# Four graph layers in one kernel: the recurrent layer's state is turned by DMA and VectorE instead of TensorE, two groups' recurrences are woven, and ScalarE takes the score's two addends

## The chip, the cores and the metric

The kernel runs on one core of a Trainium2 chip. The core has five engines that run side by side, each through its own list of instructions in the order of the list: TensorE (PE in the profile; PEld is its weight load), VectorE (DVE), ScalarE (ACT), GpSimd (POOL) and SyncE (SP), which here issues all DMA transfers. An instruction that needs a result of another engine waits, and all that stands behind it on its own engine waits with it. The metric is the device time of one execution in microseconds (us). The kernel before took 2698.12 us, the median of three runs (2695.11 to 2700.67).

## The reference

Input are 128 graphs with 128 nodes each, node rows `x` (128, 128, 256) in fp32 and an adjacency `adj` (128, 128, 128) in int32 that holds zeros and ones. Four layers follow one another, each as `x = layernorm(x + layer(x, adj))`:

```python
# layer 0: attention with 4 heads of 64
Wh = (X @ W).reshape(B, N, H, F)
e = leaky_relu(e_src[:, :, None, :] + e_dst[:, None, :, :], 0.2)   # e_src, e_dst: Wh against a_src, a_dst
alpha = softmax(where(mask, e, NEG_INF), axis=2)
Hout = elu(einsum('bijh,bjhf->bihf', alpha, Wh))
# layer 1: three rounds of a gated recurrent cell over the graph
for i in range(3):
    m = h @ weight[i]
    aggr = einsum('bst,bsd->btd', A, m)
    h = gru_cell(aggr, h, w_ih, w_hh, b_ih, b_hh)     # r, z: sigmoid; n: tanh(i_n + r*h_n); (1-z)*n + z*h
# layer 2: one weight for each relation 1..4 of adj, plus a bias
# layer 3: attention with one head of 256, as layer 0
```

The graphs are independent of one another.

## The kernel before

Graphs are handled in 33 groups: one of two graphs, 31 of four and one of two. For a group of four a tile is [128 partitions, 4 x 128 or 4 x 256].

**Stages and lanes.** Each group passes through generators, and one step of a generator is what it issues up to its next `yield`. `head` (letter h in the tables of the order) is layer 0; `reset_and_new` (p) and `new_and_update` (q) write the products of the recurrent gates; `chunk_0` and `chunk_1` (u and v) do the rest of the recurrent layer for the lower and upper 128 of the 256 state columns; `tail` (t) does layers 2 and 3; `loads` (l) fetches inputs; `constants` and `fold` (c, f) prepare weights at the start.

**The recurrent layer.** The state is kept transposed, state columns on partitions and nodes along the row: tiles `hT`, one for each half of the columns. A gate of four graphs needs a product of a 2 x 2 block matrix of weights with a 2 x 2 block matrix of states; it is done with seven block products instead of eight (the factors `f[0]` to `f[6]` on the weights, and sums `T_h`, `T_a` of state blocks made by `right_sums`, L559). One such product, L603, is written as one matmul of 128 x 256 and runs as two TensorE instructions. The gates r, ni, nh and z share three PSUM banks of the tag `sums` and three of `gate`; two banks of the tag `ps` serve all else.

For the neighbours (`neighbours`, L577) the product with the adjacency (`edge`) contracts over nodes, so it needs the state with nodes on partitions. After rounds 1 and 2 each half of the new state `hT` is therefore turned. Before the change TensorE does that for every group (`"gru": tuple(range(64))` in `BY_PE`): four transposes of 128 x 128 into one `ps` bank (L127), and a ScalarE copy to `hN` (L699). Then come four neighbour products, a ScalarE copy `agT` (L586) and VectorE differences `T_a`.

**Turning by DMA.** Elsewhere in the middle groups a tile is turned by DMA: one write to a DRAM scratch (`to_dram`), four reads that fetch 32 x 32 squares to their mirrored places (`squares`, pieces of 128 bytes), and a VectorE transpose within each 32 x 32 square. So are turned x0 (L450), the probabilities `em` to `aT` (L525, L840), `h0T`, the last state (tail, L730 and L737) and `x3T`. `BY_PE` names the first and last groups that use TensorE for this instead.

**Scores.** In layer 0 the destination scores of a group are turned into rows in DRAM (`to_rows`, L414 and L416) and read back spread over all partitions straight into `em` (`from_rows`, L424). VectorE then adds, for each graph and head, the own score (a column of `wh`) and the mask `nbias` in one instruction (L488, 16 for a group of four), and the softmax follows on `em`. `nbias` is -1e30 where there is no edge; VectorE makes it from `adj` (L433), once for layer 0 and once for layer 3, where `adj` is loaded a second time (`adj3`, L154).

**The order.** All instructions are issued in an order written out by hand in strings: `START`, then `STEPS` once for each of the 29 middle positions p, then `END`. Each letter stands for one step of one stage of a group at a distance from p (the tables `FIRST`, `PERIOD`, `LAST`). At the end of the function every instruction is tied to its predecessor on the same engine, so each engine, SP with its DMA issues too, follows the strings. In one period of `STEPS` nearly all recurrent work is of one group: of the 72 steps each of p and q, 68 and 67 are of group p, 4 and 5 of group p-1.

Of the kernel before, what the change touches and what calls it, by code (L numbers as in the profile page):

```python
# [9 lines left out]
F32 = mybir.dt.float32  # L10
BF16 = mybir.dt.bfloat16
I32 = mybir.dt.int32
# [4 lines left out]
P = 128  # L17
# [9 lines left out]
BY_PE = {"head": (0,), "rows0": (0, 1), "gru": tuple(range(64)), "rows3": (-1,), "tail": (-1, -2)}  # L27
# [26 lines left out]
FIRST = {"a": ("h", 0), "b": ("c", 0), "c": ("f", 0), "d": ("l", 1), "e": ("h", 1), "f": ("l", 0), "g": ("p", 0), "h": ("u", 0), "i": ("q", 0), "j": ("v", 0), "k": ("l", 2), "l": ("h", 2), "m": ("u", 1), "n": ("v", 1), "o": ("p", 1), "p": ("q", 1), "q": ("t", 0), "r": ("l", 3), "s": ("h", 3)}  # L54
START = """
aababbcbcaccaaccaadccacacacaccacaadaacccccccaeaaaacaacaaaaaaaaaaaeecaaaceaaeaeaeaeeaafcacaaeeaaaaghh
dcigjfchjibhggicjgijiejjigeggcgckgeeigeiggcggiigbjgeihiiigigghicjeeiigehgjgiheigiehejiechjhijccciejh
ghjihechkjiclbjjhgejihhihgiejigjggjijgiggigfjiggeigilegjighgeieggciejghiggiigehhiilhejigeehgeheejhlj
lijheigihjhiieejhjhjijhjjgieghjgejgjggeegijegliegiebgfghlgiilggigjlhgilhiggigilgiijhigejliiglhhigijl
jiiejmnminnmopjnomonnhohoplojoqoopopplpopmlpoopoqolqobnppqoooolpqpmpqopqpllmpnpmmppqoqpnoqmopqmqmmfm  # L60
dpopnqqplqnmmlnplnonmrnnmqprlqnomnlnpspopqolpqpnolqnpqqpqnnolqooopqpoqlopbpompoqnqplsplolopopsolonpm
opnommmloqmsmllloslqmmpoqpqmnmnkmpnlqnmqllqqnoopqmmnnonnnqqqosolqpspslsnploplnnqllpoolosoqnoooplsqpp
monpooppopponosommlnppppp
"""
PERIOD = {"a": ("q", -1), "b": ("p", -1), "c": ("u", -1), "d": ("h", 0), "e": ("u", 0), "f": ("v", 0), "g": ("t", -2), "h": ("h", 1), "i": ("l", 2), "j": ("v", -1), "k": ("p", 0), "l": ("h", 2), "m": ("q", 0), "n": ("t", -1), "o": ("l", -1), "p": ("t", -3), "q": ("l", 0), "r": ("l", 1)}
STEPS = """
abbcdccebfeaegefaahibjcfahkcjjkfjgilkfkkfmjmkkmkkmknmhkkmmhmkmekemfgkkmnhfmmkmkhfekkmomkhnmegmhkmkgm
mkennnengeggenhmekmenmennpnfennhenhfmmhkfemnfekffnfnnhhffmqkfmnflmmknmnffhkkkgnkmhgfmmkknkmpnmgmlhek
khhngfhfgnkmekmhkemkmhmpnmkhkkglmghnkelefenmlehhnhkmhlrnkemffnekehhffnnefhnfmefnefmnfneekkfhkhgmkhpf
mmfnhlkkfhkkfmkmmkmhlkknmmlkhnmehlgmemlffkknmkefmmnkkkmm  # L70
"""
LAST = {"a": ("t", -2), "b": ("p", -3), "c": ("q", -3), "d": ("u", -3), "e": ("h", -2), "f": ("v", -3), "g": ("h", -1), "h": ("u", -2), "i": ("v", -2), "j": ("p", -2), "k": ("t", -4), "l": ("t", -5), "m": ("q", -2), "n": ("t", -3), "o": ("l", -3), "p": ("t", -1), "q": ("l", -1), "r": ("l", -2), "s": ("u", -1), "t": ("v", -1), "u": ("p", -1), "v": ("q", -1)}
END = """
abbccdbdcdbedfgfhijfcihdhhikiclfjjjmjmjijgljfmgjjlmimmjjmmgjmhknjkmjjijmmkigmimnhjmhggjgmnmjmjhmghmg
nkkmnhjnnhggjhkjghnmkhnhmjhnnmjiniimnnihklgnhmikkhmngnniikininjmnnmiiijmnmgmoiipmnjjnjjjkgmjmjjnnkmq
gmgjjmihhpgjigjimjgmmgjjajmhgmjjngmhmjghnhmnhmgjnmighghghirniniihnhiijnhngnmmhgihikjnjijmnjimigkmgjn
gjgjijmnjimmjjmmkjgmhhjmiimghmgmjjmnirmjjnjjmmjgstjmnjmjnhmhtsimthisthmsuuiuuitvtuvvuuuvuhivuvauuuav
vusktuauuvsvavanvvvuuvnsvvutnvuasvvksnvuntusvvsnuvassnususaaatsataatnssasvvttaaaavtvtatantvtuututuuu
taukvnuvnvtauauavvavqvvauuntkvuvnnsvusuvvvuvauutauvusasautsunsvtastaavnstsasvsuatstatsttvtusqtauvsvu
tuaavtvuututnuvuvvvusuvuvsavutvvutvuvuavsuauuvvuvsusvvuatussavtttasavttppnaappppaappapppppppppppnpap  # L80
pappnapppappppppppppppappappppppapappapapaapppppppppp
# [8 lines left out]
def kernel(ctx: ExitStack, tc: tile.TileContext, a: dict, out: bass.AP):  # L90
# [43 lines left out]
    negone = cp.tile([P, 1], F32, tag="negone", name="negone")  # L134
    nc.gpsimd.memset(negone, -1.0)

    unmet = cp.tile([P, NG], F32, tag="unmet", name="unmet")
# [13 lines left out]

    def load_adj_again(st):
        st["adj3"] = sp.tile([P, st["n"], N], I32, tag="adj3", name=f"adj3_{st['g']}")
        nc.sync.dma_start(st["adj3"], adj[st["graphs"]].rearrange("g n m -> n g m"))  # L154
# [14 lines left out]
    def loads(st):  # L169
        for load in (load_x_squares, load_adj, load_rows, load_adj_squares, load_adj_again):  # L170

            if st["g"] != 0 or load in (load_adj_squares, load_adj_again):
                load(st)
            yield
# [256 lines left out]
    def absent(adj_t, name):  # L431
        nbias = ring(sp, [P, adj_t.shape[1], N], F32, "nbias", f"nbias_{name}", 2)
        nc.vector.tensor_scalar(nbias, adj_t, 0.0, NEG, ALU.is_le, ALU.mult)  # L433
        return nbias


    def head(st):
# [14 lines left out]
        nbias = absent(st["adj"], f"0_{g0}")  # L452
        yield
        if st["relations"] < R:
            above = sp.tile([P, n, N], F32, tag="rel", name=f"above_{g0}")
            nc.scalar.activation(above, st["adj"], AF.Relu, bias=negone, accum_out=unmet[:, g0 : g0 + 1])
# [16 lines left out]
        for k in range(0, G, 2):  # L473
            if k >= n:
                for _ in range(7):
                    yield
                continue
            em = ring(sp, [P, 2, H, N], F32, "em", f"em0_{g0}_{k}", 2)
            raw = {}
            for g in range(k, k + 2):  # L480
                if alone:
                    raw[g] = from_rows(bank(H, N), rows, range(g * H, g * H + H))
                else:
                    raw[g] = from_rows(em[:, g - k], rows[g])
            yield
            for g in range(k, k + 2):
                for h in range(H):
                    nc.vector.scalar_tensor_tensor(  # L488
                        em[:, g - k, h, :],
                        raw[g][:, h, :],  # L490
                        wh[:, g, D + h : D + h + 1],
                        nbias[:, g, :],
                        ALU.add,
                        ALU.add,
                    )
                yield
            blocks = em.rearrange("p g h n -> p (g h) n")
            yield from softmax_unscaled(blocks, nm, den, slice(k * H, (k + 2) * H))
            ems[k] = em if by_pe else to_dram(f"em0_{g0}_{k}", blocks)
            yield  # L500
        aTs = {}
        for k in range(0, G, 2):
            if k < n:
                aTs[k] = ring(sp, [P, 2, H, N], F32, "aT", f"aT0_{g0}_{k}", 2)
# [3 lines left out]
        y = ring(sp, [P, n, D], F32, "x1", f"x1_{g0}", 2)  # L508
# [32 lines left out]
        st["edge"] = ring(sp, [P, n, N], F32, "edge", f"edge_{g0}", 2)  # L541
# [101 lines left out]
    def chunk(st, c):  # L643

        g0, G = st["g"], st["n"]
        for l, layer in enumerate(st["layers"]):
# [34 lines left out]
            if l + 1 < L:  # L681

                by_pe = st["by_pe"]["gru"]
# [27 lines left out]
    def tail(st):  # L711
# [86 lines left out]
        nbias = absent(st["adj3"], f"3_{g0}")  # L798
# [27 lines left out]
        aT = sp.tile([P, n, N], F32, tag="aT3", name=f"aT3_{g0}")  # L826
# [129 lines left out]
```

## Time and profile before

| | |
|---|---|
| median of three runs | 2698.12 us |
| the profiled execution, its own time | 2696.64 us |
| its span, first to last instruction | 2694.8 us |
| mean granted TensorE clock | 0.992 |
| busy: PE, PEld, DVE, ACT, POOL | 98%, 85%, 81%, 66%, 34% |
| TensorE instructions | 13861 |
| DMA, queue q1: packets, share of 16 engines | 1206252, 58.0% |

Times are from one profiled execution. A busy share is the time in which at least one instruction of the engine runs; matmuls overlap one another, so TensorE's pace is read from the starts of its instructions, not from their durations. A row of a group gives count, busy time in us and mean duration in ns, then the idle time before it and what ended it. A DMA row gives the time from issue to landing.

### The profile page before, as it was taken

The numbers are of one execution on the slowest core, as the hardware profiler recorded it, in microseconds if no ns is written. First come the engines' busy times: TensorE is split into PE (matmuls) and PEld (weight loads), VectorE is DVE, ScalarE is ACT, GpSimd is POOL, SyncE is SP. The second block draws the span as 40 slices with busy tenths as digits, with TensorE's granted clock in tenths as the row PEclk, the third lists the DMA queues.
The fourth block names the chain that finished last, engine by engine and source line by source line (L and its number), as shares of the span: only waits on it lengthen the run. The fifth ranks groups of instructions, "written<-read, shape, count | busy, mean of one in ns | idle before, by whom it ended". The sixth has DMA issues, their size and how long they took to land. (4 is left out here: it accounts for less than half of the span.)

```text
span 2694.8 us, 43276 instructions
## 1 busy us (share of the span) xinstructions
PE 2635.8 (98%) x13861; PEld 2287.6 (85%) x13861; DVE 2187.5 (81%) x5059; ACT 1774.2 (66%) x4510; POOL 915.8 (34%) x923
## 2 busy tenths in 40 slices
PE   8899999999999999999999999999999999999996
PEld 5788888888888888888888888888888888888885
DVE  5777888888888888888888888888888888888875
ACT  3556666667666667766667766667766667766755
POOL 0233434333434333434233434333334333334331
PEclk8999999999999999999999999999999999999998
DMA  3455565666565666575666575665676566565521
GB/s 90 88 108 102 110 126 116 124 115 111 116 133 112 123 116 111 116 132 112 123 118 109 117 132 114 121 119 111 114 131 115 121 117 108 116 131 109 118 46 35
DMA packets 1206486, 302.31 MB, mean 112 GB/s; under 512 B 930156, under 2 KB 1190380, under 8 KB 1206252
## 3 DMA queue, kind: packets, MB, share of 16 engines
q1 hardware_dynamic: 1206252, 299.47, 58.0%
q8 instruction: 113, 1.85, 0.3%
q14 instruction: 121, 0.99, 0.1%
HBM read 192.03 MB, written 107.33 MB: 111 GB/s over the span
## 5 line engine op out<-in xcount | busy, mean ns | idle before, releaser
L603 PE MATMUL gate<-T_h,factors_h 128*128 128x256 f32 (+1 forms) x2376 | 688.4, 374 | 2.8 <-DVE gate L631 2.7
L603 PE MATMUL gate<-T_a,factors 128*128 128x256 f32 (+1 forms) x2376 | 676.8, 373 | 0.5 <-DVE gate L631 0.5
L603 PEld LDWEIGHTS gate<-T_a,factors 128*128 128x128 f32 x2376 | 444.5, 190 | 60.3 <-DVE T_a L566 2.0
L603 PEld LDWEIGHTS gate<-T_h,factors_h 128*128 128x128 f32 x2376 | 434.4, 190 | 69.8 <-issue 12.6
L603 PE MATMUL sums<-agT,factors 128*128 128x256 f32 (+1 forms) x1188 | 336.5, 377 | 1.8 <-DVE sums L623 1.6
L670 POOL TENSOR_TENSOR d<-h1T,n 128x512 f32<-128x512 f32 (+1 forms) x66 | 95.1, 1441 | 487.4 <-ACT n L667 484.8
L393 ACT ACTIVATE em<-em,nm 128x128 f32<-128x128 f32 x640 | 248.4, 398 | 7.7 <-DVE nm L390 7.6
L603 PEld LDWEIGHTS sums<-agT,factors 128*128 128x128 f32 x1188 | 217.5, 190 | 37.6 <-DVE sums L623 10.2
L667 ACT ACTIVATE n<-n,bih 128x512 f32<-128x512 f32 (+1 forms) x198 | 140.5, 709 | 135.8 <-DVE n L665 131.7
L356 ACT ACTIVATE x<-x,mr_x,rs_x 128x256 f32<-128x256 f32 x384 | 202.6, 590 | 28.7 <-DVE mr_x L351 28.7
L740 POOL TENSOR_TENSOR x<-x,x 128x512 f32<-128x512 f32 x61 | 76.5, 1274 | 366.3 <-DVE x L737 366.3
L124 PE MATMUL ps<-wh,aT 128*128 128x64 f32 (+1 forms) x1280 | 192.7, 298 | 3.0 <-DVE aT L840 2.2
L613 ACT COPY sums<-gate 128x256 f32<-128x256 f32 (+1 forms) x396 | 140.8, 355 | 83.2 <-PE gate L603 76.2
L124 PEld LDWEIGHTS ps<-wh,aT 128*128 128x128 f32 x1280 | 172.1, 194 | 21.9 <-DVE aT L840 12.3
L603 PE MATMUL gate<-agT,factors 128*128 128x256 f32 (+1 forms) x594 | 175.1, 376 | 1.1 <-ACT r L655 0.7
L655 ACT ACTIVATE r<-sums,bhalf 128x512 f32<-128x512 f32 (+1 forms) x99 | 66.1, 668 | 158.1 <-PE sums L603 158.1
L466 ACT COPY wh<-ps 128x264 f32<-128x264 f32 x128 | 47.2, 369 | 175.3 <-PE ps L124 175.2
L670 POOL TENSOR_TENSOR d<-h2T,n 128x512 f32<-128x512 f32 (+1 forms) x66 | 82.4, 1249 | 225.5 <-ACT n L667 213.0
L675 DVE SCALAR_TENSOR_TENSOR d<-z,d 128x512 f32<-128x512 f32 (+1 forms) x198 | 138.6, 700 | 25.2 <-POOL d L670 15.9
L349 POOL TENSOR_TENSOR rs_x<-rs_x,neghalf 128x4 f32<-128x4 f32 (+1 forms) x99 | 98.9, 999 | 139.0 <-DVE rs_x L348 128.6
L586 ACT COPY agT<-ps 128x512 f32<-128x512 f32 (+1 forms) x198 | 112.0, 566 | 48.9 <-PE ps L124 48.5
L343 DVE BATCH_NORM_STATS2 st_x<-x 128x6 f32<-128x256 f32 x384 | 139.6, 411 | 4.1
(165 smaller groups left out, 6134.1 us busy)
## 6 DMA issues: line engine op xcount, KB each, us to landing
em<-d_rows SPq DMA_DIRECT2D x153, 256.0 KB, 4.7
d_em<-em SPq DMA_DIRECT2D x63, 512.0 KB, 3.6
aT<-d_em SPq DMA_DIRECT2D x252, 128.0 KB, 4.3
x0s<-in_x_dram SPq DMA_DIRECT2D x248, 64.0 KB, 2.9
adj<-in_adj_dram SPq DMA_DIRECT2D x62, 256.0 KB, 3.6
x<-in_x_dram SPq DMA_DIRECT2D x31, 512.0 KB, 4.6
d_h0T<-x SPq DMA_DIRECT2D x62, 256.0 KB, 3.4
h0T<-d_h0T SPq DMA_DIRECT2D x124, 128.0 KB, 3.8
```

Source lines behind the costliest of these rows:

```text
L124: nc.tensor.matmul(ps, lhsT, rhs, start=start, stop=stop)
L343: nc.vector.bn_stats(sums[:, g, :], y[:, g, :])
L349: nc.gpsimd.tensor_tensor(rs, rs, neghalf[:, :n], ALU.pow)
L356: nc.scalar.activation(y[:, g, :], y[:, g, :], AF.Identity, bias=mr[:, g : g + 1], scale=rs[:, g : g + 1])
L393: nc.scalar.activation(em[:, r, :], em[:, r, :], AF.Exp, bias=nm[:, i : i + 1], accum_out=den[:, i : i + 1])
L586: nc.scalar.copy(t, ps)
L603: nc.tensor.matmul(into, w[:, SEL[name], k - 1], layer[source][k], start=start, stop=True, skip_group_check=True)
L613: nc.scalar.copy(c11, c21)
L667: nc.scalar.activation(n, n, AF.Tanh, bias=bih[:, 2 * C + c : 2 * C + c + 1])
L670: nc.gpsimd.tensor_sub(d, hT, n)
L675: nc.vector.scalar_tensor_tensor(d, tz, 1.0, d, ALU.add, ALU.mult)
L740: nc.gpsimd.tensor_add(y[:, k : k + 2], y[:, k : k + 2], st["x1"][:, k : k + 2])
```

## The change

- `BY_PE`: the key `gru` becomes `gru1` and `gru2`, both with groups 0, 1 and the last two. In the other 29 groups the state after rounds 1 and 2 is turned by the path that the code already had: a write of `hT` to DRAM, four reads in squares to `hN`, a VectorE transpose of 128 x 512.
- Scores of layer 0: ScalarE makes `own` (mask plus own score) by 16 instructions of 128 x 128 for a group of four, from `nbias` and `wh` alone; VectorE adds `own` to the rows with one instruction of 128 x 1024 for two graphs.
- `absent` makes `nbias` on ScalarE, for layer 0 from `adj`, for layer 3 from `edge`, which is kept longer (ring of four). The second load of `adj` goes.
- The test that `adj` holds only zeros and ones uses a Square instead of a Relu.
- `em` and `aT` share one ring of three tiles; `own` has one; `x1` has three; the layer-3 `aT3` takes the place of `em3`.
- `rows0` gets group 2: its score rows are spread by TensorE.
- A new written order. In one period, of p's 72 steps 47 are of group p and 25 of group p-1, of q's 41 and 31: the last round of one group is woven with the first rounds of the next. The tail reaches to group p-4.

```diff
-BY_PE = {"head": (0,), "rows0": (0, 1), "gru": tuple(range(64)), "rows3": (-1,), "tail": (-1, -2)}
+BY_PE = {"head": (0,), "rows0": (0, 1, 2), "gru1": (0, 1, -1, -2), "gru2": (0, 1, -1, -2), "rows3": (-1,), "tail": (-1, -2)}
...
-PERIOD = {"a": ("q", -1), "b": ("p", -1), "c": ("u", -1), "d": ("h", 0), "e": ("u", 0), "f": ("v", 0), "g": ("t", -2), "h": ("h", 1), "i": ("l", 2), "j": ("v", -1), "k": ("p", 0), "l": ("h", 2), "m": ("q", 0), "n": ("t", -1), "o": ("l", -1), "p": ("t", -3), "q": ("l", 0), "r": ("l", 1)}
+PERIOD = {"a": ("v", 0), "b": ("t", -3), "c": ("u", 0), "d": ("q", -1), "e": ("t", -2), "f": ("u", -1), "g": ("p", -1), "h": ("p", 0), "i": ("l", 2), "j": ("v", -1), "k": ("q", 0), "l": ("h", 1), "m": ("l", -1), "n": ("t", -4), "o": ("h", 2), "p": ("l", 1), "q": ("t", -1), "r": ("u", 1)}
 STEPS = """
-abbcdccebfeaegefaahibjcfahkcjjkfjgilkfkkfmjmkkmkkmknmhkkmmhmkmekemfgkkmnhfmmkmkhfekkmomkhnmegmhkmkgm
...
+abcccdeaddfgaehieadihjdkeakahhdfbflhkjdhjffmlnjhhkeelhkhehohfbljhelekjehkhkhcehjjkfcekeeahllefhnklae
...
-    negone = cp.tile([P, 1], F32, tag="negone", name="negone")
-    nc.gpsimd.memset(negone, -1.0)
+    negbig = cp.tile([P, 1], F32, tag="negbig", name="negbig")
+    nc.gpsimd.memset(negbig, NEG)
...
-    def load_adj_again(st):
-        st["adj3"] = sp.tile([P, st["n"], N], I32, tag="adj3", name=f"adj3_{st['g']}")
-        nc.sync.dma_start(st["adj3"], adj[st["graphs"]].rearrange("g n m -> n g m"))
...
-    def absent(adj_t, name):
-        nbias = ring(sp, [P, adj_t.shape[1], N], F32, "nbias", f"nbias_{name}", 2)
-        nc.vector.tensor_scalar(nbias, adj_t, 0.0, NEG, ALU.is_le, ALU.mult)
+    def absent(st, present, name):
+
+        nbias = ring(sp, [P, st["n"], N], F32, "nbias", f"nbias_{name}", 2)
+        if st["relations"] < R:
+            nc.scalar.activation(nbias, st[present], AF.Identity, bias=negbig, scale=-NEG)
+        else:
+            if present != "adj":
+                load_adj(st)
+            nc.vector.tensor_scalar(nbias, st["adj"], 0.0, NEG, ALU.is_le, ALU.mult)
         return nbias
...
-            above = sp.tile([P, n, N], F32, tag="rel", name=f"above_{g0}")
-            nc.scalar.activation(above, st["adj"], AF.Relu, bias=negone, accum_out=unmet[:, g0 : g0 + 1])
+            off = sp.tile([P, n, N], F32, tag="rel", name=f"off_{g0}")
+            nc.scalar.activation(off, st["adj"], AF.Square, bias=neghalf[:, :1], accum_out=spread[:, g0 : g0 + 1])
...
-            em = ring(sp, [P, 2, H, N], F32, "em", f"em0_{g0}_{k}", 2)
-            raw = {}
-            for g in range(k, k + 2):
-                if alone:
-                    raw[g] = from_rows(bank(H, N), rows, range(g * H, g * H + H))
-                else:
-                    raw[g] = from_rows(em[:, g - k], rows[g])
+            em = ring(sp, [P, 2, H, N], F32, "em", f"em0_{g0}_{k}", 3)
+            own = ring(sp, [P, 2, H, N], F32, "own", f"own_{g0}_{k}", 1)
+            if not alone:
+                for g in range(k, k + 2):
+                    from_rows(em[:, g - k], rows[g])
             yield
             for g in range(k, k + 2):
                 for h in range(H):
-                    nc.vector.scalar_tensor_tensor(
-                        em[:, g - k, h, :],
-                        raw[g][:, h, :],
-                        wh[:, g, D + h : D + h + 1],
-                        nbias[:, g, :],
-                        ALU.add,
-                        ALU.add,
+                    nc.scalar.activation(
+                        own[:, g - k, h, :], nbias[:, g, :], AF.Identity, bias=wh[:, g, D + h : D + h + 1]
                     )
                 yield
+            if alone:
+                for g in range(k, k + 2):
+                    raw = from_rows(bank(H, N), rows, range(g * H, g * H + H))
+                    nc.vector.tensor_add(em[:, g - k], raw, own[:, g - k])
+            else:
+                nc.vector.tensor_add(em, em, own)
+            yield
...
-                aTs[k] = ring(sp, [P, 2, H, N], F32, "aT", f"aT0_{g0}_{k}", 2)
+                aTs[k] = ring(sp, [P, 2, H, N], F32, "em", f"aT0_{g0}_{k}", 3)
...
-        st["edge"] = ring(sp, [P, n, N], F32, "edge", f"edge_{g0}", 2)
+        st["edge"] = ring(sp, [P, n, N], F32, "edge", f"edge_{g0}", 4)
...
-                by_pe = st["by_pe"]["gru"]
+                by_pe = st["by_pe"]["gru" + "12"[l]]
...
-        nbias = absent(st["adj3"], f"3_{g0}")
+        nbias = absent(st, "edge", f"3_{g0}")
```

## The prediction

> **What bounds the kernel now.** First the page's head and the stretch from 300 to 2300 us, where one period of the order follows another.
>
> ```profile
> span 2694.8 us, 43276 instructions
> PE 2635.8 (98%) x13861; PEld 2287.6 (85%) x13861; DVE 2187.5 (81%) x5059; ACT 1774.2 (66%) x4510; POOL 915.8 (34%) x923
> ...
> 300.00:2300.00 2000.00, 1989.84 (x10410) 1739.55 (x10410) 1666.97 (x3811) 1354.30 (x3410) 708.85 (x695) 1.00 0.62 118
> ```
>
> In the middle TensorE is busy 99.5% at full granted clock (1.00), VectorE 83%, ScalarE 68%, the DMA engines 62%. A busy share of overlapping matmuls could hide holes, so I went on to TensorE's timeline and read the starts.
>
> ```profile
> 973.29 0.59 PE L603 MATMUL gate<-T_h,factors_h 128*128 128x256 f32 x2
> 973.72 0.59 PE L603 MATMUL gate<-T_a,factors 128*128 128x256 f32 x2
> ...
> 976.33 0.60 PE L127 MATMUL ps<-ident,h2T 128*128 128x128 f32 x4
> 976.76 0.60 PE L603 MATMUL gate<-h2T,factors_h 128*128 128x256 f32 x2
> ```
>
> A recurrent product (two instructions) takes 0.43 us from start to start, and so do four transposes of a state half. At these spacings I count 79.2 us of TensorE for a group of four: 126 products 54.4, the projections with x0s, x3T and hr 10.5, the attention products of both layers 5.3, neighbours 5.4, relations 1.8, state transposes 1.73. The layer-3 probabilities of successive groups are turned (L840) at 201.0 to 2615.8 us in 31 instructions, 80.5 us apart. So TensorE has only some 1.4 us of holes a period: its work is the time. Of the waits of TensorE for others, the longest in all are small and scattered:
>
> ```profile
> PEld gate L603 <- PE gate L603: 16.9, 28, 0.6
> PEld sums L603 <- DVE sums L623: 16.5, 44, 1.3
> ...
> PEld ps L124 <- DVE aT L840: 12.3, 28, 0.9
> ```
>
> **The transposes of the recurrent state.** 29 groups lose four sets of four transposes: 29 x 4 x 0.435 = 50.5 us less TensorE work. Their copies (L699, 585 ns) go from ScalarE: -2.3 us a group, all beside TensorE. In their place each set gets one DMA write, four reads and a VectorE transpose of 128 x 512. The trace has exactly this shape in layer 3:
>
> ```profile
> d_h<-h3T SPq DMA_DIRECT2D x60, 256.0 KB, 2.4
> aT<-d_em SPq DMA_DIRECT2D x120, 64.0 KB, 2.2
> ...
> L840 DVE STREAM_TRANSPOSE aT<-aT 128x512 f32<-128x512 f32 x30 | 20.8, 694 | 0.0
> ```
>
> A turn of one half: the write lands in 2.4 us and the reads follow 2.7 us after it (the median of the last state's turn), four reads are issued over 1.6 us, the last lands 2.2 us later, VectorE 0.69: 7.2 us from the state's end, with nothing in front. Is it hidden? I counted from the order strings the TensorE work written between the step that makes the state and its neighbour products. Before: 4.4, 5.2, 4.8 and 4.4 us (round 1 lower and upper half, round 2 likewise). After: 14.4, 13.9, 13.9 and 12.6. The state's two VectorE instructions end some 1.6 us (712 + 889 ns) after their place, so 11.0 us or more are left for 7.2. The cover is the other group's last or first round. Without it each turn would stop TensorE for 7 us, 28 us a period.
>
> [...]
>
> **The queues that the turns join.** SP gets 20 issues more a group (0.36 to 0.41 us each) and one less: +8 us on a queue that mostly waits. What matters is what stands in front. Two places are tight.
>
> Round 1, lower half: its reads stand behind the upper half's write, whose state is written 7.0 us after the lower one; 7.0 + 1.6, a write issue 0.4, reads 1.6, landing 2.2 and VectorE 0.7 make 13.5, against 14.4 written. VectorE is the later one here. Behind the layer-3 score rows (their last column block is written at 3.0, VectorE's turn of it ends near 4.5, the row below shows that the spread lands about 2.0 + 4.7 us after the rows' issue) it starts the scores at 11.2. Then come the scores (4 x 345 ns), the slope and maximum (652 + 686), a scaling (687) and the state's transpose (694): 3.45 + 0.69 = 4.1 us, or 3.6 back to back (all rows of VectorE add up to some 78 us a period, their busy time to 67). That ends at 14.8 to 15.3: 0.4 to 0.9 us late.
>
> ```profile
> 1061.44 0.53 SPq L416 DMA_DIRECT2D d_rows<-turned  x1
> 1062.01 0.47 SPq L854 DMA_DIRECT2D out_dram<-o  x1
> 1063.39 0.36 SPq L424 DMA_DIRECT2D em<-d_rows  x1
> ```
>
> Round 2, upper half: state at 52.7 us after the first round's, neighbours at 65.3. Its reads stand behind a write of `em`, which waits for eight exponentials (8 x (398 + 196) = 4.75 us, with a copy of 0.6 among them, to 58.1), and behind two spreads (issued over 1.8): 60.2, reads to 61.9, landing 64.1 alone or 66 among the large reads (`aT<-d_em` of 128 KB takes 4.3), VectorE 0.7: 0.5 us early to 1.5 late.
>
> **VectorE and ScalarE.** The scores:
>
> ```profile
> L488 DVE SCALAR_TENSOR_TENSOR em<-em,wh,nbias 128x128 f32<-128x128 f32 x488 | 135.4, 343 | 0.0
> L393 ACT ACTIVATE em<-em,nm 128x128 f32<-128x128 f32 x640 | 248.4, 398 | 7.7 <-DVE nm L390 7.6
> L433 DVE TENSOR_SCALAR nbias<-adj 128x512 f32<-128x512 int32 x62 | 40.8, 659 | 0.0
> L456 ACT ACTIVATE above<-adj,negone 128x512 f32<-128x512 int32 x31 | 22.0, 709 | 0.0
> ```
>
> VectorE loses 16 x 0.343 = 5.5 us and gains two adds of 128 x 1024, 1.23 each as L389; two masks go (-1.3), four transposes come (+2.8): -1.6 a group. So it stays near 66 us of some 79. ScalarE's 16 new instructions have no row; between a copy of 128 x 128 from PSUM (L613, 262 ns) and the exponential of that shape from SBUF with a bias (398), I take 0.39, as it too reads SBUF with a bias: +6.2 (bounds 4.2 to 6.4). The masks cost as L456, +1.4; the copies went. Net +5.3, so ScalarE goes from 54 to some 60 us, 75%. Both lie beside TensorE, and `own` is written ahead of the rows' arrival: after it only one add of 1.23 us is left where 8 x 0.343 = 2.7 were. If that cover failed, the 20 us between the `em` write and its reads take it.
>
> **Smaller edits.** Group 2's rows by TensorE: 32 instructions at 0.112 and one transpose, +3.7 us, counted in full. Square for Relu: none, the same row. The dropped load: one SP issue and some 0.5% of the packets; the turns add 29 x 4 x 2560 pieces, 297,000 to 1,206,252, so the DMA share goes from 58% to about 72%. The shared rings: each reuse that I followed lies 20 us or more behind its last reader (`own`: the add of the pair before, 14 us). Gate banks: between a bank's last reader and the next gate's first product the old order has 0.0 to 1.8 us at its closest, the new 0.9 to 1.8; nothing is added.
>
> **The sum**, against the profiled execution's 2696.6 us (1.5 under the median): -50.5 + 3.7 = 2649.8 with the holes as they are. For the two tight places I take 0.6 us a period together (the middle of 0.4 to 0.9 at the first, none at the second, whose early end is as near). Times 28: +17. Forecast 2667.
>
> **Rivals.** *More than the sum.* The old order's 1.4 us of holes shrink too: up to 0.4 a period (one recurs in front of a product with h1T), -11, so 2639 to 2650. For it: the wider gate-bank distances. Against: VectorE gets denser in places.
>
> *Slower.* One mechanism: round 2's upper half sits in SP's queue behind the `em` write, and its reads land late because the DMA engines, 62% busy now, go to some 76%. It decides once TensorE stands 46.8 / 28 = 1.67 us a period longer than before. With 1.5 at that place and 0.9 at round 1 the time is 2649.8 + 28 x 2.4 = 2717; with one more us at each, 2773. For it: SP's order is fixed, and a wait there holds everything behind it. Against: the last state's turn, twice as large, already ends within 8.7 us of its state under load.
>
> *No change.* VectorE sets the period in TensorE's place: its 66 us of work would have to string out to 80, as chains through ScalarE and back can make it; the gain is eaten to 2692 to 2702.
>
> **How the numbers follow.** Likeliest, both tight places within their bounds (0 to 1.5 us a period): 2650 to 2692, 0.53. More than the sum: 0.16. No change, within the 0.2% (5 us) that a measurement of this kernel can tell: 0.05. Slower 0.26. Faster is 0.53 + 0.16 = 0.69. The range leaves out 0.04 below 2638 and 0.16 of the slower case above 2712; the likeliest alone is 2650 to 2692.
>
> **What would show it.** TensorE 431 instructions fewer (464 gone, 33 new); periods of 78.5 to 79.5 us; no h1N or h2N copies on ScalarE in the middle; an idle time of TensorE's weight loads in front of the neighbours that a VectorE transpose of h1N ended, 0.4 to 0.9 us each; DMA about 72%. I am wrong if TensorE waits there for the DMA itself, if the periods are longer than 80.5, or if start and end lose more than 10 us by the deeper weave, of which I count nothing: the work written after the last recurrent product is 13 us in both orders.

## The result, and the profile after

The changed kernel takes 2705.89 us (median of 20 runs) against 2695.11 for the kernel before on the same chip: a ratio of 1.0044, 95% interval 1.0032 to 1.0056. It is 0.44% slower. The forecast of 2667 was 39 us too low and on the wrong side.

The head of the page of the kernel after, and its DMA queue:

```profile
span 2704.4 us, 43742 instructions
...
PE 2602.6 (96%) x13430; PEld 2270.7 (84%) x13430; DVE 2208.9 (82%) x4666; ACT 1856.7 (69%) x4973; POOL 897.6 (33%) x923
...
q1 hardware_dynamic: 1494872, 350.87, 67.5%
```

TensorE has 431 instructions fewer, as forecast, and yet the span is 9.6 us longer. The windows of the kernel after, for the middle and for three short stretches (length; busy us and instructions of PE, PEld, DVE, ACT, POOL; granted clock; DMA share; GB/s), show how:

```profile
300.00:2300.00 2000.00, 1956.90 (x10013) 1715.34 (x10012) 1695.64 (x3518) 1414.81 (x3772) 698.40 (x696) 0.99 0.74 141
1008.00:1013.00 5.00, 5.00 (x36) 4.53 (x34) 3.73 (x5) 2.60 (x8) 1.63 (x2) 1.00 0.67 109
1013.00:1019.00 6.00, 4.64 (x16) 3.69 (x15) 4.90 (x11) 2.87 (x10) 0.16 (x1) 0.72 0.90 201
1019.00:1025.00 6.00, 6.00 (x33) 5.40 (x32) 4.57 (x10) 3.42 (x7) 2.40 (x2) 1.00 0.61 154
```

TensorE now stands still for 43 us of these 2000, where it stood for 10. From 1013 to 1019 it has lost 1.4 us, and the granted clock is 0.72; before and behind that it is 1.00.

How much is lost where is read from the starts of TensorE's instructions, as in the prediction: whatever lies between two starts beyond the usual spacing of that pair of shapes (0.216 us for a 128 x 256 half of a product, 0.110 to 0.112 for transposes and attention products, and so on) is counted as a hole. From 500 to 2100 us, some 20 periods, this gives 30.1 us before and 69.9 after: 1.5 and 3.5 us a period. The 69.9 are 25.2 in front of `sums<-agT` (place 1), 17.8 in front of `gate<-T_a` (place 2), about 14.6 where products follow each other at twice the usual spacing, and 12.3 of small pieces. Two us a period in some 28 periods are 56 us of new holes, against 47 of work that went: the 9.6 of the span. A period, from one `h1T` to that of the next group, is 80.7 us long on average in both kernels, where I had forecast 78.5 to 79.5. Of the 57 us of holes more in the whole span, 41.7 lie in 24 middle periods, 14.6 behind them (the last four groups: the same two places, and one wait of TensorE for `h3T`, 5.2 us long) and 0.6 ahead of them: the deeper weave costs next to nothing at the start.

**Place 1.** The timeline of the kernel after (start, duration, engine, line, tiles; in brackets the idle time and what ended it; the rows between those shown are left out):

```profile
1011.12 0.64 DVE L665 SCALAR_TENSOR_TENSOR n<-r,n 128x512 f32<-128x512 f32 x1
1011.28 1.97 PE L124 MATMUL ps<-wh,aT 128*128 128x64 f32 x16
1013.07 1.14 DVE L822 SCALAR_TENSOR_TENSOR em<-em,wh,nbias 128x128 f32<-128x128 f32 x4 [1.30 <-DMA em<-d_rows]
1014.13 0.42 DVE L625 TENSOR_TENSOR sums<-gate,p_ni 128x256 f32<-128x256 f32 x1
1014.60 0.90 PE L605 MATMUL sums<-agT,factors 128*128 128x256 f32 x2 [1.35 <-DVE sums L625]
1015.29 1.06 PE L605 MATMUL gate<-T_a,factors 128*128 128x256 f32 x2
1016.15 1.06 PE L605 MATMUL sums<-h2T,factors_h 128*128 128x256 f32 x2
```

VectorE comes to the scores of layer 3 (L822) and their rows have not landed. It stands for 1.30 us. Behind the scores in its list is the first add of gate ni (L625, 0.42 us), which needs TensorE's products and a copy of earlier ones (`p_ni`) but not the rows, and TensorE's next product needs that add. TensorE stands for 1.35 us. The products behind the hole start at 1015.29 and 1016.15: 0.86 us apart, twice the usual 0.43.

**Place 2.** The timeline of the kernel after, at another place of the period (rows between those shown are left out):

```profile
835.15 0.68 DVE L376 SCALAR_TENSOR_TENSOR elu<-o,elu 128x512 f32<-128x512 f32 x1
835.74 2.95 POOL L672 TENSOR_TENSOR d<-h0T,n 128x512 f32<-128x512 f32 x2 [9.79 <-ACT n L669]
835.87 1.70 DVE L377 SCALAR_TENSOR_TENSOR o<-elu,x 128x512 f32<-128x512 f32 x1
837.49 0.42 DVE L633 TENSOR_TENSOR gate<-gate,p_z 128x256 f32<-128x256 f32 x1
837.82 0.41 DVE L568 TENSOR_TENSOR T_a<-ps,agT 128x256 f32<-128x256 f32 x1
838.15 0.41 DVE L568 TENSOR_TENSOR T_a<-ps,T_a 128x256 f32<-128x256 f32 x1
838.28 0.70 PE L605 MATMUL gate<-T_a,factors 128*128 128x256 f32 x2 [0.69 <-DVE T_a L568]
```

VectorE does not wait for anything here; it has too much in a row. The ELU of layer 3 (L376, L377) stands in front of z's add and of the differences `T_a`, and L377 takes 1.70 us, while GpSimd runs beside it. The same line in the kernels before and after, from their views by source line (min/median/max in ns):

```profile
L381 DVE SCALAR_TENSOR_TENSOR o<-elu,x x64: 691/692/1100, 233.6 to 2685.3; 128x512 f32<-128x512 f32 x64
```

```profile
L377 DVE SCALAR_TENSOR_TENSOR o<-elu,x x64: 691/1113/1711, 274.4 to 2695.0; 128x512 f32<-128x512 f32 x64
```

The waits of TensorE and of VectorE for other engines, in the kernel after (us in all, times, longest), list the two places, the new state transposes last:

```profile
PEld sums L605 <- DVE sums L625: 38.7, 40, 2.1
...
DVE em L822 <- DMA em<-d_rows: 36.1, 32, 3.2
...
PEld gate L605 <- DVE T_a L568: 35.3, 55, 1.1
...
PEld ps L124 <- DVE h2N L703: 8.2, 26, 0.5
```

**The turned states themselves** hold nobody up for long: those 8.2 us are 0.3 for each of 26, and 0.5 at most. The view of the transpose's own line, after:

```profile
L703 DVE STREAM_TRANSPOSE h1N<-h1N x58: 679/699/712, 215.5 to 2476.8; 128x512 f32<-128x512 f32 x58
...
DMA h1N<-d_h: 0.8, 1
```

VectorE waited for the DMA of a turn once in the whole run, for 0.8 us.

### The profile page after: what moved, and what is told of

Read it like the earlier page. It is cut to its first block, busy times and chain, and to the rows that moved or that the text cites. A ratio compares the mean times of both kernels' runs of the same rounds, so it can differ in the third digit from the quotient of the medians.

```text
span 2704.4 us, 43742 instructions
## 1 busy us (share of the span) xinstructions
PE 2602.6 (96%) x13430; PEld 2270.7 (84%) x13430; DVE 2208.9 (82%) x4666; ACT 1856.7 (69%) x4973; POOL 897.6 (33%) x923
## 3 DMA queue, kind: packets, MB, share of 16 engines
q1 hardware_dynamic: 1494872, 350.87, 67.5%
## 5 line engine op out<-in xcount | busy, mean ns | idle before, releaser
L605 PE MATMUL gate<-T_a,factors 128*128 128x256 f32 (+1 forms) x2376 | 689.3, 378 | 24.7 <-DVE T_a L568 19.2
L605 PE MATMUL gate<-T_h,factors_h 128*128 128x256 f32 (+1 forms) x2376 | 680.9, 375 | 3.2 <-DVE gate L633 3.1
L605 PEld LDWEIGHTS gate<-T_a,factors 128*128 128x128 f32 x2376 | 436.6, 192 | 97.4 <-DVE T_a L568 35.3
L605 PEld LDWEIGHTS gate<-T_h,factors_h 128*128 128x128 f32 x2376 | 442.8, 191 | 67.1 <-DVE gate L633 5.5
L605 PE MATMUL sums<-agT,factors 128*128 128x256 f32 (+1 forms) x1188 | 356.7, 383 | 30.0 <-DVE sums L625 29.7
L665 DVE SCALAR_TENSOR_TENSOR n<-r,n 128x512 f32<-128x512 f32 (+1 forms) x198 | 147.1, 744 | 82.6 <-ACT n L663 81.6
L672 POOL TENSOR_TENSOR d<-h0T,n 128x512 f32<-128x512 f32 (+1 forms) x66 | 92.6, 1423 | 328.8 <-ACT n L669 328.8
L488 ACT ACTIVATE own<-nbias,wh 128x128 f32<-128x128 f32 x512 | 162.9, 398 | 0.0
L672 POOL TENSOR_TENSOR d<-h1T,n 128x512 f32<-128x512 f32 (+1 forms) x66 | 109.7, 1661 | 101.1 <-ACT n L669 101.1
L124 PE MATMUL ps<-w,x0s 128*128 128x264 f32 x512 | 138.2, 394 | 2.7 <-issue 1.4
```

Of the source, the lines that this page charges most:

```text
L124: nc.tensor.matmul(ps, lhsT, rhs, start=start, stop=stop)
L488: nc.scalar.activation(own[:, g - k, h, :], nbias[:, g, :], AF.Identity, bias=wh[:, g, D + h : D + h + 1])
L605: nc.tensor.matmul(into, w[:, SEL[name], k - 1], layer[source][k], start=start, stop=True, skip_group_check=True)
L665: nc.vector.scalar_tensor_tensor(n, tr, 1.0, n, ALU.add, ALU.mult)
L672: nc.gpsimd.tensor_sub(d, hT, n)
```

## The experiments

The theory after the comparison: the recurrent turn is covered; the time is lost where VectorE's list holds up an add that TensorE needs, at place 1 behind rows that are not there yet, at place 2 behind a stretched ELU. The rivals: the DMA engines are crowded and deliver late (then fewer transfers must help); the woven order itself is the loss and the turn is free; VectorE is full, so that moving one thing out of the way only moves the hole. In the diffs of the order a line stands for one letter of `STEPS`, with its number, stage and position (t -3 is the tail of group p-3), and what it issues. All ratios are against the kernel before on the same chip (2695 to 2698 us).

### 1. The layer-3 scores behind ni's first add

```diff
-217 t -2  scores of layer 3 (L822)
 218 p -1  ni: first add (L625)
+217 t -2  scores of layer 3 (L822)
```

> One letter of the period is moved: VectorE's layer-3 score instruction, which waits for the spread rows, is written behind the add of gate ni of the group before instead of in front of it. Theory A (VectorE stands in front of that add waiting for the rows; TensorE stands behind it, 25.2 us over 20 periods in the changed kernel, and the granted clock drops after the longer of these holes): most of 1.2 us a period and of the clock's 0.7 goes, 28 x 1.4 = 40 us, time 2666 (2646 to 2686); no hole in front of the product sums<-agT that follows ps<-wh,aT. Rival B (the crowded DMA queues are what is short, the rows only show it): the hole comes again a few instructions later, 2696 to 2710.

Measured: 2694.33 us, ratio 0.9989 (0.9979 to 0.9999); 11.6 us faster than the changed kernel. Holes from 500 to 2100 us: 54.4. The waits of this kernel:

```profile
PEld gate L605 <- DVE gate L633: 53.8, 38, 2.6
...
DVE em L822 <- DMA em<-d_rows: 32.8, 32, 3.4
...
PEld sums L605 <- DVE sums L625: 5.5, 12, 0.7
```

The wait for ni's first add fell from 38.7 to 5.5 us, and the stretches at twice the spacing went with it (granted clock from 300 to 2300 us 1.00, against 0.99). VectorE still waits for the rows just as long (32.8), and now what comes next behind the scores is late: ni's second add (L633). So place 1 is as read, but a swap in the order only hands the hole to the next add in the list: 11.6 us came back of the 40 expected. Of the holes from 500 to 2100 us 15.5 are gone, about as much as the 14.6 of the stretches at twice the spacing: what came back is for the most part the clock, and the hole itself only changed its place.

### 2. The differences of round 2 ahead of the ELU

```diff
+158 v -1  differences T_a, round 2 (L568)
 151 t -3  first ELU pair of layer 3 (L376, L377)
 ...
-158 v -1  differences T_a, round 2 (L568)
```

> One letter of the period is moved: VectorE's second neighbour differences of round 2's upper half are written in front of the layer-3 ELU pair instead of behind it. Theory A (TensorE's regular hole of 0.85 us in front of gate<-T_a is VectorE's order: the ELU pair, 1.7 us where GpSimd works beside it, stands in front): 0.85 us a period goes, 28 x 0.85 = 24, time 2682 (2674 to 2694). Rival B (the upper half's turn lands late, and the difference waits for the neighbours' product): nothing moves, 2700 to 2710.

Measured: 2735.21 us, 1.0134 (1.0116 to 1.0152). The 17.8 us in front of `gate<-T_a` go; in their place comes a hole of 1.78 us a period in front of `gate<-T_h`, behind z's second add, 35.5 us in 20 periods. VectorE's stretch there is full: what is put first is in time, and what is put back is later than it was.

### 3. Both moves

```diff
+158 v -1  differences T_a, round 2
 151 t -3  first ELU pair of layer 3
...
-217 t -2  scores of layer 3
 218 p -1  ni: first add
+217 t -2  scores of layer 3
```

> Both letters moved. Theory A: the two holes are independent, 40 + 24 us, time 2642 (2622 to 2665), which is faster than the kernel before by 1 to 3%. Rival B: 2690 to 2710.

Measured: 2715.44 us, 1.0070 (1.0056 to 1.0083). Added up, -11.6 of the first and +29.3 of the second would make +17.7 over the changed kernel; +9.6 was measured, so most of both effects is there, and the difference is not explained.

### 4. The new order with the states turned by TensorE

```diff
-"gru1": (0, 1, -1, -2), "gru2": (0, 1, -1, -2)
+"gru1": tuple(range(64)), "gru2": tuple(range(64))
```

> The changed kernel and its order, but every group's state is turned by TensorE and ScalarE again. TensorE gets back 50.5 us of work. Theory A: without the turns' transfers the rows land about 0.7 us sooner, so the hole in front of ni's add shrinks from 1.2 to some 0.5 and the clock does not drop, 28 x 1.4 = 39 less; the regular 0.85 stays: 2706 + 50 - 39 = 2717 (2700 to 2735). Rival C (all of the lost gain is due to the DMA turn and the order itself is free of holes): 2706 + 50 - 56 = 2700 or less.

Measured: 2798.03 us, 1.0383 (1.0363 to 1.0403), 81 us above what was expected. The windows of the middle and the waits of this kernel:

```profile
300.00:2300.00 2000.00, 1921.76 (x10035) 1684.61 (x10033) 1580.61 (x3294) 1419.14 (x3728) 673.40 (x671) 1.00 0.57 111
```

```profile
PEld ps L124 <- ACT h2N L701: 48.9, 30, 2.8
PEld sums L605 <- DVE sums L625: 37.8, 39, 1.9
...
DVE em L822 <- DMA em<-d_rows: 34.8, 32, 3.1
```

The DMA engines carry 57% instead of 74%, and the layer-3 rows are as late as with the turns (34.8 us in 32 waits; 36.1 with them). So the crowding that the turns bring is not why VectorE waits for the rows. What this kernel loses beside the 50.5 us of transposes shows in the first line: in the new order ScalarE is late with the copy to `h2N`. No run took that wait away.

### 5. The ELU pair behind both differences and r's product

```diff
-151 t -3  first ELU pair of layer 3
...
 160 p -1  r, round 2: seventh product
+151 t -3  first ELU pair of layer 3
 161 t -2  transpose of x3T (L325)
```

> One letter of the changed order is moved: the layer-3 ELU pair of VectorE goes behind both the neighbour differences and the second add of gate z, directly in front of the transpose of x3T. Theory A (that pair stands in front of what TensorE needs next; the run with the differences alone moved lost 1.78 us a period in front of the product behind z's add instead): the hole of 0.85 in front of gate<-T_a goes and no 1.78 comes, 28 x 0.85 = 24 us under the changed kernel's 2706, so 2682 (2672 to 2694). Rival D (VectorE has too much work around there whatever its order): a hole of 0.5 to 1 us comes in front of the projection with x3T, 2696 to 2710.

Measured: 2723.74 us, 1.0104 (1.0084 to 1.0124). The hole is now in front of the projection with `x3T`, 1.14 us a period:

```profile
PEld ps L124 <- DVE x3T L325: 37.2, 27, 1.4
```

Third order of the same instructions, third victim. At place 2 the rival that VectorE is full is right: nowhere in this stretch is there a gap in its list to put the ELU into.

### 6. The same, with the scores behind both adds of ni

```diff
-151 t -3  first ELU pair of layer 3
 160 p -1  r, round 2: seventh product
+151 t -3  first ELU pair of layer 3
...
-217 t -2  scores of layer 3
-221 t -2  maximum of layer 3
 229 p -1  ni: second add
+217 t -2  scores of layer 3
 230 u  0  transpose of h1N
+221 t -2  maximum of layer 3
```

> As the run before, and the layer-3 score instructions go behind both adds of gate ni, the slope and maximum behind the turned state's transpose. Theory A: both holes of the period go, the longer one with its clock drop: 24 + 28 x 1.9 = 77 us under 2706, so 2629 (2615 to 2660), which is faster than the kernel before by 1.3 to 3%. Rival B (the late rows hold up whatever VectorE does next): a third of that, 2670 to 2700.

Measured: 2759.68 us, 1.0235 (1.0218 to 1.0252). The hole in front of the projection with `x3T` stays (1.1 us a period), and that of ni's adds goes on to z's adds (1.2 in front of `sums<-h2T`, 0.6 in front of `gate<-T_h`) and to the neighbours of `h1N` (0.5).

### 7. The kernel before with only the turn by DMA

```diff
-"gru": tuple(range(64))
+"gru": (0, 1, -1, -2)
```

> The kernel before with its own order and scores; only the state's turn goes by DMA and VectorE in the 29 middle groups. The order leaves 4.4 to 5.2 us of TensorE work for it. Theory A (cover is what makes the turn cheap): each of four turns a period is late by 8.8 - 4.4 to 5.2 = 3.6 to 4.4 us, some of it shared between the halves: 8 to 17 us a period, 2650 + 28 x 12 = 2990 (2870 to 3130). Rival E (the turn is covered by TensorE's slack elsewhere): 2650 to 2700.

Measured: 3177.3 us in a single run, 187 more than expected and 47 above the range given; the granted clock in the middle, 0.94, is part of that. Waits of this kernel:

```profile
DVE h1N L701 <- DMA h1N<-d_h: 281.6, 58, 7.3
...
PE ps L124 <- DVE h1N L701: 241.0, 58, 6.7
```

This is the direction of the prediction's "Without it each turn would stop TensorE for 7 us", at a smaller size: VectorE waits up to 7.3 us for the DMA, against 0.8 once in the new order, and TensorE behind it 4.2 us on average (241.0 in 58) in round 1 and less in round 2, since the old order has 4.4 to 5.2 us of cover; in all it costs 17 us a period, not 28. With experiment 4 there are four kernels to compare (median us; that at the top right is a single run). "Old order" stands for the kernel before in all else, "new order" for the kernel after, with its scores and masks too:

| | state turned by TensorE | by DMA and VectorE |
|---|---|---|
| old order | 2695 | 3177 |
| new order | 2798 | 2706 |

In the new order the turn is worth 92 us, in the old one it costs 482. Neither half of the change can be judged without the other.

### 8. The own score back on VectorE

```diff
-nc.scalar.activation(own[:, g - k, h, :], nbias[:, g, :], AF.Identity, bias=wh[:, g, D + h : D + h + 1])
...
-nc.vector.tensor_add(em, em, own)
+nc.vector.scalar_tensor_tensor(em[:, g - k, h, :], em[:, g - k, h, :], wh[:, g, D + h : D + h + 1], nbias[:, g, :], ALU.add, ALU.add)
```

> The changed kernel and order with the score's two addends on VectorE again (eight instructions for two graphs at the place of the one add, none on ScalarE). VectorE gets 2 x (2.7 - 1.2) = 3 us a period more, ScalarE 6.2 less. Theory A (VectorE's order makes the holes): slower, 0.5 to 2 us a period, 2706 + 35 = 2741 (2715 to 2765). Rival F (ScalarE's 16 new instructions delay the chains): faster than the changed kernel, 2670 to 2695.

Measured: 2771.19 us, 1.0266 (1.0245 to 1.0286), 30 us above the expected time and just above its range. In the new order the score's move to ScalarE is worth 65 us: 2.3 us a period, for 16 x 0.343 - 2 x 1.23 = 3.0 us a period of VectorE's time. Waits of this kernel:

```profile
PEld sums L615 <- DVE sums L635: 96.0, 68, 2.4
```

Three parts in four of VectorE's added time reach the end, and the 6 us or so a period that ScalarE is spared bring nothing that shows: this speaks for VectorE as the engine that sets the pace beside TensorE, and against rival F.

### 9. The ELU where VectorE has nothing to do

In the changed kernel VectorE is idle a third of the time in the 3 us in which it waits for the layer-3 rows, and a tenth at most in the 12 us around place 2. So the ELU moves from the one to the other: its first pair some 50 steps later, its second behind ni's first add, and the scores behind that.

```diff
-151 t -3  first ELU pair of layer 3
...
+151 t -3  first ELU pair of layer 3
 202 t -3  layer norm of that half
...
-203 t -3  second ELU pair of layer 3
...
-217 t -2  scores of layer 3
 218 p -1  ni: first add
+203 t -3  second ELU pair of layer 3
+217 t -2  scores of layer 3
```

> The changed order with the two layer-3 ELU pairs moved back: the first from the full stretch before the transpose of x3T to the place of the second, the second behind the add of gate ni, where VectorE waits for the rows; the scores follow it. Theory A (VectorE's queue is full for 14 us before the x3T transpose and idle 1 us a period before the scores): the regular 0.85 us hole goes and none comes in front of x3T, 28 x 0.85 = 24 under the run with the scores moved alone (2694), and up to 0.6 a period comes back behind the scores: 2680 (2665 to 2692). Rival D (the lost time only moves along VectorE's queue): 2694 to 2715.

Measured: 2679.07 us, ratio 0.9927 (0.9901 to 0.9952): faster than both kernels, 0.7% under the one before. VectorE's timeline in this kernel, and its lines of the view by source line and of the waits:

```profile
1007.14 0.65 DVE L665 SCALAR_TENSOR_TENSOR n<-r,n 128x512 f32<-128x512 f32 x1
1007.71 0.43 DVE L625 TENSOR_TENSOR sums<-gate,p_ni 128x256 f32<-128x256 f32 x1
1008.04 0.68 DVE L376 SCALAR_TENSOR_TENSOR elu<-o,elu 128x512 f32<-128x512 f32 x1
1008.76 0.69 DVE L377 SCALAR_TENSOR_TENSOR o<-elu,x 128x512 f32<-128x512 f32 x1
1009.37 1.13 DVE L822 SCALAR_TENSOR_TENSOR em<-em,wh,nbias 128x128 f32<-128x128 f32 x4
```

```profile
L377 DVE SCALAR_TENSOR_TENSOR o<-elu,x x64: 691/693/1107, 274.7 to 2667.8; 128x512 f32<-128x512 f32 x64
```

```profile
PE gate L605 <- DVE gate L633: 50.5, 37, 2.4
...
DVE em L822 <- DMA em<-d_rows: 11.3, 7, 3.6
```

VectorE has work until the rows are there: 7 waits instead of 32. L377 of the second pair takes 0.69 us at its new place, where GpSimd is idle; that of the first takes 1.10 beside GpSimd, where the second stood before, instead of 1.70. Periods are 79.7 us on average. TensorE's wait for `T_a` at place 2, 19.2 us in the kernel after and in experiment 1, is gone, and its wait for ni's second add (L633), behind the scores' slope, their maximum and a scaling, has grown from 38.8 in experiment 1 to 50.5. So the time came back at place 2, as expected, and not behind the rows: of the 46.0 us of holes left from 500 to 2100 us, 33.7 are in front of what needs that add. Of the 27 us under the kernel after, 12 are experiment 1's move, which this kernel holds too. The rest of the edit does two things at once, fills idle time and takes the ELU away from GpSimd; the runs don't tell their shares apart.

### 10 to 12. Three tries at the last hole

Each starts from experiment 9 and puts ni's second add ahead of what stands before it.

10, the scores behind both adds, the maximum behind z's first add, the exponentials (with the empty step behind them, 237) later:

```diff
-217 t -2  scores of layer 3
-221 t -2  maximum of layer 3
 229 p -1  ni: second add
+217 t -2  scores of layer 3
-235 t -2  exponentials of layer 3
 240 q -1  z, round 2: first add
+221 t -2  maximum of layer 3
 247 v -1  tanh of round 2
+235 t -2  exponentials of layer 3
```

> As the run before; besides, the scores stand behind both adds of gate ni, and the slope and maximum behind gate z's first add, the exponentials later with them. Theory A: TensorE no longer waits behind the scores or the maximum for a gate's add; 2655 (2635 to 2680). Rival D: the delayed scores push the turned state and the neighbours, as in the run with the scores behind both adds (2760): 2700 to 2760.

Measured: 2789.62 us, 1.0336 (1.0310 to 1.0362). Holes of 2.3 us a period in front of `gate<-T_h`, 1.2 in front of `gate<-T_a`.

11, only the maximum behind the state's transpose:

```diff
-221 t -2  maximum of layer 3
 230 u  0  transpose of h1N
+221 t -2  maximum of layer 3
```

> As the run with the ELU pairs moved back (2679), and the layer-3 slope and maximum go behind the second add of gate ni and the transpose of the turned state. There TensorE still stood 1.68 us a period in front of the product behind that add. Theory A: the add comes 0.9 us sooner, the turned state 0.5, gate z's add 0.5 later: 28 x 0.6 = 17, 2662 (2645 to 2675). Rival D (the time only moves along VectorE's queue): 2672 to 2700.

Measured: 2723.36 us, 1.0099 (1.0083 to 1.0115). The one hole becomes three: 1.1 us a period in front of `sums<-h2T` (z's first add), about 1.0 in front of `gate<-T_a`, 0.7 in front of `gate<-T_h`.

12, as 11, with the scaling and the relu of layer 0 behind z's add and an add of round 2 as well, and an SP write behind the upper half's transpose:

```diff
-226 h +1  scaling of the second pair, layer 0
-233 u -1  add of round 2
-238 h +1  relu of layer 0
 240 q -1  z, round 2: first add
+233 u -1  add of round 2
+226 h +1  scaling of the second pair, layer 0
+238 h +1  relu of layer 0
...
-255 t -2  write of em3 (SP)
 258 v  0  transpose of h1N
+255 t -2  write of em3 (SP)
```

> As the run before, and besides the attention scaling goes behind gate z's add and the write of the layer-3 probabilities behind the upper half's transpose, so that VectorE takes the gates' adds first. Theory A: the hole of 1.68 us shrinks to some 0.4 at one place: 28 x 1.3 = 36, 2643 (2630 to 2662). Rival D: 2672 to 2710.

Measured: 2728.85 us, 1.0125 (1.0110 to 1.0141). All three came out above experiment 9, and 135, 61 and 86 us above what I expected: I took the hole that I saw away and did not see the next. A wait that hides behind another is not in the profile until the first is gone. Whether there is an order that comes near the 2650 of "holes as they are" stays open.

## Why the prediction was wrong

**The work that goes (-50.5 + 3.7): right.** 431 instructions fewer, and with 56.9 us of holes more in a span 9.6 longer some 47 us of work are gone, as forecast. **The cover of the turn: right.** 11 us were counted against 7.2; VectorE waited for the DMA of a turn once (0.8 us), and experiment 7 shows up to 7.3 us where the cover is short.

**The two tight places, 0.6 us a period together: this step failed.** At round 2's upper half I took nothing, and 0.3 us were measured (8.2 us in 26 waits); the rival that saw SP's queue and the DMA engines fail there, from 1.67 us a period on, didn't occur. At round 1 the place was right and the mechanism too: VectorE is late behind the layer-3 rows. They arrive 7.5 us after they are turned (1005.6 to 1013.1), where I had 6.7. But I followed one thing behind the scores, the state's transpose, with 14 us of cover. My list there (scores, slope and maximum, a scaling, the state's transpose) left out the two adds of gate ni that stand in the same queue. They have hardly any cover: between the last product that the first one adds and the product that needs it, TensorE has 16 attention products, 16 x 0.111 = 1.8 us. So the late rows cost 1.26 us a period where I had 0.4 to 0.9 at another tile, and experiment 1 shows that it is the queue: move that add ahead and its wait goes (38.7 to 5.5 us), while the next add takes over the hole. (The list's sum, 3.45 us, should be 3.41; that changes nothing.)

**"With the holes as they are" failed a second time, at place 2,** which I had not listed. 17.8 us in 20 periods are 0.9 a period. My VectorE balance said -1.6 us a group; from 300 to 2300 us its durations add up to 1900 us instead of 1886, 14 more, where -1.6 a period would have been 40 less. The parts were right: 5.5 us of scores and 1.3 of masks went, the adds (1222 ns) and transposes (692 to 703) came at the prices taken. What was missing is that the same instructions take another time at their new places: `o<-elu,x` 1409 ns on average instead of 692 (+34.5 us), `n<-r,n` 773 instead of 684 (+14.0), the relations 865 instead of 427 (+11.4) and `h2T` 896 instead of 692 (+10.2), while `h1T`, `h3T` and layer 0's `x<-elu,x` fell from 900 to 692 (-31 together).

**A term that was not there:** the granted clock, 0.992 to 0.981. The stretches at twice the spacing are 0.7 us a period, a third of the two us. **The end,** where I counted nothing, has 14.6 us of holes more; so the prediction's sign of being wrong, more than 10 us at start and end, was there, though about half of it is the same two places.

**The sizes beside it were right:** `own` at 398 ns against 0.39 taken; ScalarE's durations add up to 5.9 us a period more, against 5.3; 67.5% of DMA share against 72%, and 74% in the middle against 76%. The last shows no consequence for the layer-3 rows (experiment 4).

**The rivals.** "No change, VectorE sets the period" was the nearest in its mechanism, at a chance of 0.05 and with 2692 to 2702 us. I looked at it as a sum, 66 of 80 us, and a sum of 83% says that there is room. Experiments 2, 5 and 6 show that in the 12 us around place 2 there is none, while the idle time lies elsewhere, at a wait that stands in front of urgent work. The slower case came by another mechanism than the one that its rival names.

How far each part is settled: that the queue behind the late rows makes the wait at place 1 is shown by experiment 1, that the turns' transfers don't by experiment 4. Place 2's being full is shown by 2 and 5, and that the ELU pair in it costs the time by 9. That GpSimd stretches the ELU is read from the trace's instructions without an exception (below), but no run took GpSimd away alone.

## What to carry to other kernels

When a change puts latency under cover, list every instruction that stands behind the first late one in each engine's queue, and give each its own slack: the victim is the one with the least, not the one that the change is about. A busy share of 83% is room only where the idle time lies; work moved out of a full stretch into the engine's own wait (experiment 9 against experiment 1) brought 15 us, while moving urgent work ahead of less urgent work in a full stretch only chose another victim. Two halves of a change that cover each other, here the order and the turn, have no separate prices: take both from the pair.

## What the runs showed of the hardware

**VectorE and GpSimd.** The trace of the kernel after has 128 instructions of L377 (two fp32 inputs in SBUF, 128 x 512). The 73 with no GpSimd instruction beside them take 691 to 694 ns, each of them; the 55 with one beside them take 1096 to 1711. Of the same kind are `n<-r,n` (675 alone, 1164 on average for the 33 that share more than 0.1 us with GpSimd) and `h2T<-d,n` (692 and 1100). L376 (`elu<-o,elu`, two inputs too) is hit less: 684 alone, 833 to 847 in the 27 that run wholly beside GpSimd's `T_h<-h1T`. The gates' adds, with one of their two inputs in PSUM, do not change: they take 0.42 both ways. Of the instructions with one input the maximum (1220 ns) and the transposes of 128 x 1024 (1.23 us) do not change, but the relations do, a comparison of int32 with a number: at 128 x 512 two take 427 and 428 ns alone, the 29 beside GpSimd 842 to 873. The slope L385 reads one tile as both inputs and at 128 x 1024 is hardly hit: 1.21 us alone, 1.24 on average beside GpSimd, once 1.67. On L377 the size is up to 1.02 us on 0.69. Why some of these instructions take longer beside GpSimd and others do not was not shown.

**The clock after a short hole.** Of 20 periods from 500 to 2100 us in the kernel after, nine have a stretch of about 3 us behind place 1 at 0.86 instead of 0.43 us between products, at a cost of 1.6 us each on average (14.6 in all). The holes in front of them add up to 1.4 to 2.1 us; holes of 0.7 to 1.0 us by themselves were never followed by one, and two of 1.57 and 1.78 us were not either (that of 1.78 at 772.7, with the clock at 1.00 behind it).

What tells the holes with a drop from those without is settled only in part. In the clock records of this trace each of these nine drops is 3.41 us at 0.50 (one is twice as long), and all begin on one grid of 3.41 us: those at 1015.0, 1096.9, 1178.8 and 1260.7 us stand 24 steps apart. In front of each of the nine, at least 1.4 us of holes fell into the one interval of the grid that ends where the drop begins; a hole of 1.57 us that ended at 1343.2 was cut by the grid into two intervals with 1.06 and 0.70 us, and no drop came. But the hole that began at 772.7 lay whole in one interval (1.88 us of holes) without a drop, and the kernel of experiment 1, where TensorE stands up to 2.4 us in front of `gate` products behind L633 (38.8 us in 37 waits of the whole run), has a granted clock of 1.00 from 300 to 2300 us, against 0.99 here. What else decides stays open.
